# Cross-attention with LayerNorm: an input-ordered prologue, values placed by multiplication, the LayerNorm shift on GpSimd, another order in the epilogue

## The chip, the cores and the metric

The kernel runs on one NeuronCore of a Trainium2 chip. The metric is the device time of one execution in microseconds; the runs before the change gave 656.06, 656.39 and 652.27 (median 656.06). Engines are named as in the profile: PE is TensorE (PEld its weight loads), DVE VectorE, ACT ScalarE, POOL GpSimd, SP the engine that issues most DMAs.

## What is computed

Four batches of 2048 queries with 512 features attend to 77 context rows each; 16 heads of 32 features. gamma and beta are drawn at random.

```
qs = (x @ wq) in heads;  ks = (ctx @ wk) in heads;  vs = (ctx @ wv) in heads
scores = qs ks^T / sqrt(32);  scores = where(mask, -inf, scores)
attn = softmax(scores) @ vs
out = attn @ wo + x
result = (out - mean(out)) / sqrt(var(out) + 1e-5) * gamma + beta
```

## The kernel before

**Tiles and blocks.** 8192 query rows make 64 tiles of 128 rows, and two tiles make a block of 256 (32 blocks); a batch has 16 tiles. The order of every instruction is written out by hand: the loop `for u in range(NT + 8)` issues, in one turn u, pieces of different tiles. Each engine works through its own instructions strictly in that order.

**Precision.** A matmul operand in fp32 is split in two fp32r parts, high (a cast on ACT) and low (a subtraction, on DVE or GpSimd), and each product is three matmuls: high x high, high x low, low x high. `split` does it for weights and inputs.

**One turn u of the loop, in order.**
- `load_xT(b)` loads the transposed inputs of a later block (SP, and a casting DMA on GpSimd's queue); `load_x(u-5)` loads the residual rows.
- `shift` (L362, DVE): minus mean times reciprocal deviation, for the two tiles of a block, every second turn.
- `scores(u)`: 12 matmuls on PE (L249), then 16 DVE instructions (L252) that add the mask bias, negate and reduce, one per head, from PSUM.
- `av_evac` (odd u: ah on ACT L321, al on DVE L322), `q_evac` (qh on ACT L149, ql on DVE L150); at the end of a batch `kblocks` (kbh on ACT L174, kbl on DVE L175) puts the next batch's keys in a block-diagonal layout.
- `scale` (L372, ACT) for two finished tiles, then `exps(u)`: 16 exps on ACT (L266) with sums.
- `transp(u-1)`: a DVE transpose of the probabilities (L287); each second turn `regroup`: 12 DMAs on SP (L298) that place them as PT for the value products.
- `split_xT` (GpSimd L122), `affine` (GpSimd L376, L377: gamma and beta).
- `o_proj(u-6)` (PE L338), `av` (even u, PE L307: 32 small matmuls per block), `q_half` (PE L139: 24 matmuls), in that order on PE.
- `stats(u-6)`: residual add (L344), bn_stats (L346), aggregate (L351), variance plus epsilon (L357) on DVE and the power -1/2 on GpSimd (L358), for two tiles at once in odd turns.
- `normalise(u)`: reciprocal of the sums on DVE (L278), multiplication of the probabilities on GpSimd (L281).
- stores. The last four tiles (TAILV) are scaled by DVE (L369, L370) instead.

**Heads in pairs.** Probabilities of a pair of heads lie side by side, 154 columns padded to 160. Transposed in blocks of 32, head 1 of a pair begins 77 columns in, so its keys come out rotated; the value rows and the key order of odd heads must match that. vsb has 96 rows per batch: 77 keys and 19 more (TAIL_K) that repeat the tail for odd heads, and zero rows where a head has nothing.

**Prologue.** Inputs x and wq arrive in four chunks of 128 features, then ctx and wk, all on SP's queue. q of block 0 is computed by output group (each needs all four chunks), then the keys (`keys`), then the loop begins. Value weights are split by GpSimd. In turns 1 and 2 `values` computes the values of 308 context rows in three groups of up to 128 rows regardless of the batch, copies them from PSUM (ACT L189), and 16 small DMAs on SP (L196) place them in vsb, which GpSimd has set to zero (L386).

**Buffers.** PSUM has 8 banks, used in rotation by all matmul results. `o` tiles have 4 buffers, so stats of tile t waits for the store of tile t - 4; xtf has one buffer.

Of the kernel before, what the change touches and what calls it, by code (L numbers as in the profile page):

```python
# [40 lines left out]
def xattn_layernorm(  # L41
# [38 lines left out]
    bet = const.tile([P, D], F32, name="bet")  # L80
    mhalf = const.tile([P, 2], F32, name="mhalf")
    pbuf = [const.tile([P, NP, PW], F32, name=f"pbuf{i}") for i in range(NPB)]

    stage_a = sb.tile([P, 2, NC_D, D], F32, tag="PT", name="stage_a")
    stage_b = sb.tile([P, 2, NC_D, D], F32, tag="PT", name="stage_b")
    ctx_t = sb.tile([P, NC_D, NB * NK], F32, tag="B", name="ctx_t")
    ctx_f = [ctx_t[:, c] for c in range(NC_D)]
    ctx_2 = sb.tile([P, 2, NC_D, NB * NK], F32R, tag="B", name="ctx_s")
    ctx_s = [ctx_2[:, i] for i in range(2)]
    wvh = [sb.tile([P, D], F32R, tag="o", bufs=4, name=f"wvh{c}") for c in range(NC_D)]  # L90
    wv2 = [sb.tile([P, 2, D], F32R, tag=t, name=f"wvl{t}") for t in ("AH", "AL")]
    wvl = [wv2[c // 2][:, c % 2] for c in range(NC_D)]

    def wview(w, c):
        return w[c * P : (c + 1) * P, :]

    def split(hi, lo, src, eng=nc.vector):
        nc.scalar.copy(hi, src)
        eng.tensor_tensor(lo, src, hi.bitcast(F32), ALU.subtract)  # L99

# [4 lines left out]
    nmax, sums, bts, at, pas = {}, {}, {}, {}, {}  # L105
    xr, od, pos, mvs, rns = {}, {}, {}, {}, {}


    def load_xT(b):
        f = sb.tile([P, NC_D, BLK], F32, tag="xtf", bufs=1, name=f"xtf_{b}")  # L110
        h = sb.tile([P, NC_D, BLK], F32R, tag="xth", bufs=3, name=f"xth_{b}")
        nc.sync.dma_start(f, xT[b])
        if b == 1:
            nc.scalar.copy(h, f)
        else:
            nc.gpsimd.dma_start(h, xT[b])
        blk[b] = [h, f]

    def split_xT(b):
        h, f = blk[b]  # L120
        l = sb.tile([P, NC_D, BLK], F32R, tag="xtl", name=f"xtl_{b}")
        nc.gpsimd.tensor_tensor(l, f, h.bitcast(F32), ALU.subtract)  # L122
        blk[b] = [h, l]
# [28 lines left out]

    def keys():
        for m in range(NG):
            pk = bank(f"pk_{m}")
            ms = slice(m * P, (m + 1) * P)
            n = 0
            for c in range(NC_D):
                for w, i in ((woh, 0), (woh, 1), (wol, 0)):
                    nc.tensor.matmul(  # L160
                        pk[:, : NB * NK], w[:, c, ms], ctx_s[i][:, c, :], start=(n == 0), stop=(n == 11)
                    )
                    n += 1
            pkb = pk[:, : NB * NK].rearrange("p (b k) -> p b k", b=NB)
            nc.scalar.activation(kct[:, m, :, TAIL_K:], pkb, AF.Copy, scale=KSCALE)
            nc.scalar.copy(kct[:, m, :, :TAIL_K], kct[:, m, :, NK:])
            kblocks(0, slice(m, m + 1))

    def kblocks(b, ms=slice(0, NG)):
        for j in range(GH):  # L170
            q = slice(HD * j, HD * (j + 1))
            cs = slice(NK * j, NK * (j + 1))
            src = kct[q, ms, b, keys_of(j)]
            nc.scalar.copy(kbh[q, ms, cs], src)  # L174
            nc.vector.tensor_tensor(kbl[q, ms, cs], src, kbh[q, ms, cs].bitcast(F32), ALU.subtract)  # L175


    def values(r0):
        w = min(P, NB * NK - r0)
        pv = bank(f"pv_{r0}")  # L180
        n = 0
        for c in range(NC_D):
            for i, v in ((0, wvh), (0, wvl), (1, wvh)):
                nc.tensor.matmul(
                    pv[:w, :], ctx_s[i][:, c, r0 : r0 + w], v[c], start=(n == 0), stop=(n == 11)
                )
                n += 1
        vt = sb.tile([P, D], F32, tag="xr", bufs=3, name=f"vt_{r0}")
        nc.scalar.copy(vt[:w], pv[:w])  # L189
        for b in range(NB):  # L190
            lo, hi = max(r0, b * NK), min(r0 + w, (b + 1) * NK)
            for a, k0, k1, p0 in ((0, 0, NK, 0), (1, 0, NK - TAIL_K, 0), (1, NK - TAIL_K, NK, NK)):
                u0, u1 = max(lo, b * NK + k0), min(hi, b * NK + k1)
                if u0 < u1:
                    d0 = u0 - b * NK - k0 + p0
                    nc.sync.dma_start(  # L196
                        vsb[d0 : d0 + u1 - u0, b, :].rearrange("p (q a d) -> p q a d", a=2, d=HD)[:, :, a, :],
                        vt[u0 - r0 : u1 - r0, :].rearrange("p (q a d) -> p q a d", a=2, d=HD)[:, :, a, :],
                    )

    def load_wv():
        for c in range(NC_D):
            nc.sync.dma_start(stage_b[:, 0, c], wview(wv, c))
            nc.gpsimd.dma_start(wvh[c], wview(wv, c))
        for c in range(NC_D):
            nc.gpsimd.tensor_tensor(wvl[c], stage_b[:, 0, c], wvh[c].bitcast(F32), ALU.subtract)

# [17 lines left out]

    def mask_bias(b):
        mb, nz, m8 = bat[b]
        nc.vector.tensor_scalar(mb[:, :, TAIL_K:], m8, MASKED, None, ALU.mult)
        nc.vector.tensor_copy(mb[:, :, :TAIL_K], mb[:, :, NK:])

# [61 lines left out]
    def regroup(b):  # L292
        pt = pts[b] = sb.tile([P, 4, 2, NP * 2 * 32], F32, tag="PT", name=f"PT_{b}")
        bt = bts.pop(b).rearrange("p c q t r -> p c (q t r)")
        for c in range(3):
            src = bt[:, 2:3].to_broadcast((P, 2, NP * 2 * 32)) if c == 2 else bt[:, c : c + 4 : 3]
            for i in range(4):
                nc.sync.dma_start(pt[32 * c : 32 * c + 32, i], src[32 * i : 32 * i + 32])  # L298

# [41 lines left out]
    def stats(t):  # L341
# [10 lines left out]
        nz = bat[t // TPB][1]  # L352
        lone = t >= NT - 2
        if lone or tt == 1:
# [3 lines left out]
            nc.gpsimd.tensor_tensor(rn[:, 0, j], rn[:, 0, j], mhalf[:, j], ALU.pow)  # L358

    def shift(b):  # L360
        mv, rn = mvs[b], rns[b]
        nc.vector.scalar_tensor_tensor(rn[:, 1, :], mv[:, :, 0], -1.0, rn[:, 0, :], ALU.mult, ALU.mult)  # L362

# [18 lines left out]

    nc.gpsimd.memset(mhalf, -0.5)
    nc.gpsimd.memset(kbh.bitcast(F32), 0.0)
    nc.gpsimd.memset(kbl.bitcast(F32), 0.0)
    nc.gpsimd.memset(vsb, 0.0)  # L386
    for pb in pbuf:
# [9 lines left out]
    x0l = sb.tile([P, NC_D, BLK], F32R, tag="xtl", name="xtl_0")  # L397
    blk[0] = [x0h, x0l]
    for c in range(NC_D):
        nc.sync.dma_start(x0f[:, c], xT[0, :, c])  # L400
        nc.sync.dma_start(stage_a[:, 0, c], wview(wq, c))
        split(x0h[:, c], x0l[:, c], x0f[:, c], nc.gpsimd)
        split(wqh[:, c], wql[:, c], stage_a[:, 0, c])
    for c in range(NC_D):
        nc.sync.dma_start(ctx_f[c], ctxT[:, c].rearrange("p b k -> p (b k)"))
        nc.sync.dma_start(stage_a[:, 1, c], wview(wk, c))
    load_mask(0)
    for c in range(NC_D):
        split(ctx_s[0][:, c], ctx_s[1][:, c], ctx_f[c], nc.gpsimd if c == NC_D - 1 else nc.vector)
        split(woh[:, c], wol[:, c], stage_a[:, 1, c])  # L410
    q_half(0, 0)
    q_half(0, 1)
    q_evac(0, 0)
    q_evac(0, 1)
    load_xT(1)
    split_xT(1)
    load_wv()
    keys()
    mask_bias(0)
    mask_nan(0)  # L420

    evac = []

    load_xT(2)
    for u in range(NT + 8):
        odd = u % 2
# [6 lines left out]
        ln = [f for f in (u - 8, u - 7) if not odd and 0 <= f < NT - TAILV]  # L433
        if ln:
            shift(ln[0] // 2)
        if u < NT:
            scores(u)
        if odd and 0 <= (u - 5) // 2 < NBLK:
            av_evac((u - 5) // 2)
        for q in evac:  # L440
# [5 lines left out]
        if u < NT:  # L446
            exps(u, 0, 16)
        if 0 <= u - 1 < NT:
            transp(u - 1)
            if not odd:  # L450
                regroup((u - 1) // 2)
# [14 lines left out]
        b = (u - 4) // 2  # L466
        if not odd and 0 <= b < NBLK:
            av(b)
        for r in {1: (0, P), 2: (2 * P,)}.get(u, ()):
            values(r)  # L470
        evac = [(1, 0), (1, 1)] if u == 0 else [divmod(u + 3, 2)]
        evac = [q for q in evac if q[0] < NBLK]
# [4 lines left out]
        if u == 0:  # L477
            load_wo()
            split_xT(2)
        if 2 <= u <= 3:  # L480
            split_wo(2 * u - 4)
            split_wo(2 * u - 3)
        if u < NT:
            normalise(u)
        if o >= NT - TAILV and o < NT and (o % 2 or o >= NT - 2):
            for f in (o,) if o >= NT - 2 else (o - 1, o):
                scale(f)
                store(f)
        if odd and 0 <= u - 9 < NT - TAILV:
# [47 lines left out]
```

## Time and profile before

| what | before |
|---|---|
| median of three runs | 656.06 us |
| the profiled execution, its own time | 654.69 us |
| its span, first to last instruction | 652.9 us |
| mean granted PE clock | 0.955 |
| busy PE / DVE / ACT / POOL | 89% / 84% / 74% / 66% |
| L362, the shift on DVE: 30 instructions | 64.1 us busy, 20.1 us idle before |
| L281, normalise on GpSimd: 64 | 144.0 us busy, 2251 ns each |
| L358, power on GpSimd, 128x2: 33 | 24.5 us busy |
| q, 1536 matmuls of 256 columns (L139) | about 0.118 us apart at full clock |

A line of a timeline reads: start in us from the span's start, duration, engine (a q behind it means its queue of DMA issues), line of the kernel, operation, output <- inputs, shapes, count, and in brackets the idle time of the engine before it with what ended that. Windows give busy time of each engine in a stretch, then the granted clock of PE, the mean busy share of the 16 DMA engines, and GB/s. PE's busy time overlaps from one matmul to the next, so it overstates the load; distances between starts are better.

In the page's last three slices of 40 (some 49 us) PE's busy share falls to 7, 6 and 3 tenths, and the granted clock is 7 tenths.

### The profile page before, as it was taken

What the parts mean: (1) busy time and instruction counts of PE and PEld (TensorE: products, weight loads), DVE (VectorE), ACT (ScalarE), POOL (GpSimd) and SP (SyncE); (2) the same over time, 40 slices, a digit from 0 to 9 for tenths busy, and PEclk for the clock granted to TensorE, in tenths of its full rate; (3) what the DMA queues carried; (4) which work ended last, traced back from release to release, by engine and by line L of the source; (5) the groups of instructions that cost most, each with busy time, mean ns of one, the idle gap of its engine ahead of it and who ended that gap; (6) DMA issues with size and microseconds to landing.
All of it is one profiled execution on the core that took longest, in us unless ns stands there. A gap on an engine that the chain in (4) does not pass through costs nothing.

```text
span 652.9 us, 15185 instructions
## 1 busy us (share of the span) xinstructions
PE 580.5 (89%) x4190; PEld 489.9 (75%) x4190; DVE 550.9 (84%) x2631; ACT 483.7 (74%) x2293; POOL 431.3 (66%) x303
## 2 busy tenths in 40 slices
PE   8897499998999999998999999998999999998763
PEld 5896288887888888887888777887788777886442
DVE  5768188989998888999998888999998888898836
ACT  5499197777887777777887777777887777777710
POOL 5761456776578777776578777776578777765551
PEclk8899599998999999998999999998999999998777
DMA  8483976787757777787758777777757777556663
GB/s 264 144 259 66 235 198 172 208 233 209 201 142 209 208 208 209 207 230 213 193 135 224 209 208 205 212 224 222 195 140 212 210 209 208 143 147 162 169 171 112
DMA packets 68462, 126.11 MB, mean 193 GB/s; under 512 B 14746, under 2 KB 16282, under 8 KB 68378
## 3 DMA queue, kind: packets, MB, share of 16 engines
q1 hardware_dynamic: 62954, 107.31, 60.4%
q0 software_dynamic: 5424, 17.83, 8.9%
q8 instruction: 34, 0.56, 0.4%
q14 instruction: 50, 0.41, 0.2%
HBM read 57.36 MB, written 16.78 MB: 114 GB/s over the span
## 4 chain that ended last, share of the span: by engine, by line
DVE 53%; ACT 23%; PE 10%; issue 5%; POOL 4%; SPq 3%; DMA 2%; DVEq 0%; POOLq 0%; ACTq 0%
ACT pbuf L266 19%; DVE pbuf L252 12%; DVE rn L362 10%; DVE B L287 8%; DVE al L322 5%; PE pq L139 5%; DVE st L346 4%; POOL rn L358 4%; DVE o L344 3%; DVE ql L150 3%; ACT o L372 3%; SPq L298 2%; PE pa L307 1%; DVE kbl L175 1%; DVE nm L252 1%
## 5 line engine op out<-in xcount | busy, mean ns | idle before, releaser
L266 ACT ACTIVATE pbuf<-pbuf,nm 128x77 f32<-128x77 f32 x1024 | 352.1, 350 | 8.8 <-DVE nm L252 8.1
L266 ACT ACTIVATION_READ_ACCUMULATOR pbuf<-pbuf,nm 128x1 f32 x1024 | 194.9, 190 | 0.0
L281 POOL TENSOR_TENSOR pbuf<-pbuf,ri 128x1232 f32<-128x1232 f32 x64 | 144.0, 2251 | 55.5 <-DVE ri L278 51.0
L252 DVE CUSTOM_DVE_ANT_0 pbuf<-sc,mb 128x77 f32<-128x77 f32 x1024 | 164.9, 230 | 13.2 <-PE sc L249 13.2
L139 PE MATMUL pq<-xth,wqh 128*128 128x256 f32 x512 | 148.6, 290 | 20.7 <-DVE nm L252 19.3
L139 PE MATMUL pq<-xth,wql 128*128 128x256 f32 x512 | 146.0, 285 | 0.4 <-DVE wql L99 0.4
L139 PE MATMUL pq<-xtl,wqh 128*128 128x256 f32 x512 | 145.9, 285 | 0.0
L139 PEld LDWEIGHTS pq<-xth,wqh 128*128 128x128 f32 x512 | 98.7, 193 | 36.3 <-PE pa L307 29.3
L372 ACT ACTIVATE o<-o,rn 128x512 f32<-128x512 f32 x60 | 45.7, 808 | 106.9 <-DVE rn L362 106.9
L338 PE MATMUL po<-woh,ah 128*128 128x512 f32 x256 | 106.7, 417 | 7.5 <-DVE o L344 5.6
L338 PE MATMUL po<-woh,al 128*128 128x512 f32 x256 | 105.4, 412 | 2.5 <-DVE al L322 2.5
L338 PE MATMUL po<-wol,ah 128*128 128x512 f32 x256 | 104.7, 409 | 0.0
L287 DVE STREAM_TRANSPOSE B<-pbuf 128x1280 f32<-128x1280 f32 x64 | 96.0, 1500 | 8.0 <-POOL pbuf L281 7.9
L139 PEld LDWEIGHTS pq<-xtl,wqh 128*128 128x128 f32 x512 | 98.4, 192 | 1.8 <-POOL xtl L99 0.6
L139 PEld LDWEIGHTS pq<-xth,wql 128*128 128x128 f32 x512 | 98.3, 192 | 1.3 <-DVE wql L99 1.3
L358 POOL TENSOR_TENSOR rn<-rn,mhalf 128x2 f32<-128x2 f32 (+1 forms) x33 | 24.5, 743 | 111.7 <-DVE rn L357 111.7
L122 POOL TENSOR_TENSOR xtl<-xtf,xth 128x1024 fp32r<-128x1024 f32 x31 | 74.6, 2407 | 23.5 <-DMA xtf<-xT 11.4
L376 POOL TENSOR_TENSOR o<-o,gam 128x512 f32<-128x512 f32 x60 | 77.6, 1293 | 14.6 <-ACT o L372 14.6
L249 PE MATMUL sc<-kbl,qh 128*128 128x308 f32 x256 | 78.2, 305 | 6.7 <-DVE kbl L175 6.7
L307 PE MATMUL pa<-PT,vsb 96*32 96x256 f32 x1024 | 65.3, 398 | 19.9 <-DMA vsb<-vt 14.5
L252 DVE DVE_READ_ACCUMULATOR2_ANT nm<- 128x1 f32 x1024 | 82.3, 80 | 0.0
L377 POOL TENSOR_TENSOR o<-o,bet 128x512 f32<-128x512 f32 x60 | 78.9, 1315 | 4.7
(70 smaller groups left out, 976.3 us busy)
## 6 DMA issues: line engine op xcount, KB each, us to landing
PT<-B SPq DMA_DIRECT2D x384, 128.0 KB
xr<-x SPq DMA_DIRECT2D x64, 256.0 KB
out<-o SPq DMA_DIRECT2D x64, 256.0 KB
xtf<-xT SPq DMA_DIRECT2D x31, 512.0 KB
xth<-xT POOLq DMA_DIRECT2D x30, 512.0 KB, 4.6
stage_a<-wq SPq DMA_DIRECT2D x4, 256.0 KB
stage_a<-wk SPq DMA_DIRECT2D x4, 256.0 KB
stage_b<-wv SPq DMA_DIRECT2D x4, 256.0 KB
```

The costliest lines, as they stand in the source:

```text
L122: nc.gpsimd.tensor_tensor(l, f, h.bitcast(F32), ALU.subtract)
L139: nc.tensor.matmul(pq[:, i * BLK : (i + 1) * BLK], w[:, c, ms], r[:, c, :], start=(n == 0), stop=(n == 11))
L249: nc.tensor.matmul(sc[:, :GW], a[:, g, rs], k[:, g, :], start=(n == 0), stop=(n == 2))
L252: nc.vector.tensor_tensor_reduce(pb[:, h // 2, (h % 2) * NK : (h % 2 + 1) * NK], sc[:, j * NK : (j + 1) * NK], mb[:, t % TPB, keys_of(h)], ...
L266: nc.scalar.activation(pb[:, h // 2, (h % 2) * NK : (h % 2 + 1) * NK], pb[:, h // 2, (h % 2) * NK : (h % 2 + 1) * NK], AF.Exp, bias=nmax[t ...
L281: nc.gpsimd.tensor_tensor(pv, pv, rv.to_broadcast((P, NP, 2, NK)), ALU.mult)
L287: nc.vector.transpose(bts[b][:, :, :, tt, :].rearrange("p c q r -> p q c r"), pbuf[t % NPB].rearrange("p q (c r) -> p q c r", c=5),)
L307: nc.tensor.matmul(pas[b][g // 2][HD * j : HD * (j + 1), (g % 2) * BLK : (g % 2 + 1) * BLK], vsb[:, 2 * b // TPB, HD * h : HD * (h + 1)], ...
L338: nc.tensor.matmul(po, a[:, c, rs], w[:, c, :], start=(n == 0), stop=(n == 11))
L362: nc.vector.scalar_tensor_tensor(rn[:, 1, :], mv[:, :, 0], -1.0, rn[:, 0, :], ALU.mult, ALU.mult)
L376: nc.gpsimd.tensor_tensor(o, o, gam, ALU.mult)
L377: nc.gpsimd.tensor_tensor(o, o, bet, ALU.add)
```

## The change

- **Prologue, loads.** ctx comes in two DMAs on ACT's queue, with 96 rows per batch (the 19 tail keys repeated, made on the host), ahead of the weights of the keys on SP. Block 1's inputs are loaded early, without the casting DMA.
- **Prologue, order of work.** q of block 0 accumulates chunk by chunk in four banks, as chunks arrive. The keys accumulate in two halves of the chunks. All low parts of splits go to DVE (four of x and one of ctx were on GpSimd, as were block 1's and the value weights'). q_half(1, 0) moves ahead of the loop. The evacuation of the keys alternates between ACT and DVE, and the tail keys are taken from PSUM by DVE. Before the loop, the mask bias is made for the first tile alone; the other tiles' follows in turn 0, mask_nan in turn 1.
- **Values.** One group of 96 rows per batch (turns 1, 2, 3 and 3), evacuated by two DVE multiplications with a column of ones and zeros (`vm`), which `value_rows` makes. No DMAs, no zeroed vsb.
- **Shift.** Two 128x2 multiplications on GpSimd right behind the power (times the reciprocal deviation, times -1), in `stats`.
- **Epilogue.** The last four tiles get their own power each, and are scaled and stored each in its own turn. Half of the last regroup's 12 DMAs are issued by ACT. `av` of the last block and its evacuation move from turn 66 and 67 to turn 67, behind `o_proj(61)`.

```diff
@@ stats
-        lone = t >= NT - 2
+        lone = t >= NT - TAILV
...
             nc.gpsimd.tensor_tensor(rn[:, 0, j], rn[:, 0, j], mhalf[:, j], ALU.pow)
-
-    def shift(b):
-        mv, rn = mvs[b], rns[b]
-        nc.vector.scalar_tensor_tensor(rn[:, 1, :], mv[:, :, 0], -1.0, rn[:, 0, :], ALU.mult, ALU.mult)
+            if not lone:
+                nc.gpsimd.tensor_tensor(rn[:, 1, :], mv[:, :, 0], rn[:, 0, :], ALU.mult)
+                nc.gpsimd.tensor_tensor(rn[:, 1, :], rn[:, 1, :], mneg, ALU.mult)
@@ regroup
-                nc.sync.dma_start(pt[32 * c : 32 * c + 32, i], src[32 * i : 32 * i + 32])
+                eng = nc.scalar if b == NBLK - 1 and i % 2 else nc.sync
+                eng.dma_start(pt[32 * c : 32 * c + 32, i], src[32 * i : 32 * i + 32])
@@ values
+    def values(b):
+        pv = bank(f"pv_{b}")
         n = 0
         for c in range(NC_D):
             for i, v in ((0, wvh), (0, wvl), (1, wvh)):
+                nc.tensor.matmul(pv[:NK2, :], ctx_s[c][i][:, b, :], v[c], start=(n == 0), stop=(n == 11))
                 n += 1
+        vd[b] = pv
+
+    def values_evac(b):
+        pv = vd.pop(b)[:NK2].rearrange("p (q a d) -> p q a d", a=2, d=HD)
+        for a in range(2):
+            nc.vector.tensor_scalar(
+                vsb[:, b].rearrange("p (q a d) -> p q a d", a=2, d=HD)[:, :, a], pv[:, :, a], vm[:, a, 0:1], None, ALU.mult
+            )
@@ prologue
+    for c in range(0, NC_D, 2):
+        nc.scalar.dma_start(ctx_f[:, c : c + 2], ctxT[:, c : c + 2])
     for c in range(NC_D):
         nc.sync.dma_start(stage_a[:, 1, c], wview(wk, c))
     load_mask(0)
+    load_xT(1, False)
+    value_rows()
+    pq0 = [bank(f"pq_0_{m}") for m in range(NG)]
     for c in range(NC_D):
+        split(x0h[:, c], x0l[:, c], x0f[:, c])
+        split(wqh[:, c], wql[:, c], stage_a[:, 0, c])
+        for m in range(NG):
+            for n, (w, r) in enumerate(((wqh, x0h), (wqh, x0l), (wql, x0h))):
...
+    for c in range(NC_D):
+        split(ctx_s[c][0], ctx_s[c][1], ctx_f[:, c])
         split(woh[:, c], wol[:, c], stage_a[:, 1, c])
+    for m in range(NG):
+        split(qd[0][0][:, m], qd[0][1][:, m], pq0[m][:, :BLK])
+    pks = [bank(f"pk_{m}") for m in range(NG)]
+    for m in range(NG):
+        keys_part(pks, m, (0, 1))
+    for m in range(NG):
+        keys_part(pks, m, (2, 3))
+    nc.scalar.copy(blk[1][0], blk[1][1])
+    split_xT(1)
+    q_half(1, 0)
+    mask_bias(0, slice(0, 1))
+    load_wv()
+    for m in range(NG):
+        keys_evac(pks, m)
     load_xT(2)
@@ the loop
-    for u in range(NT + 8):
+    for u in range(NT + 7):
...
-        if not odd and 0 <= b < NBLK:
+        if not odd and 0 <= b < NBLK - 1:
             av(b)
-        for r in {1: (0, P), 2: (2 * P,)}.get(u, ()):
-            values(r)
+        if u == NT + 3:
+            av(NBLK - 1)
+            av_evac(NBLK - 1)
+        for v in {1: (0,), 2: (1,), 3: (2, 3)}.get(u, ()):
+            values(v)
...
-        if o >= NT - TAILV and o < NT and (o % 2 or o >= NT - 2):
-            for f in (o,) if o >= NT - 2 else (o - 1, o):
-                scale(f)
-                store(f)
+        if NT - TAILV <= o < NT:
+            scale(o)
+            store(o)
```

## The prediction

> **What bounds the kernel now.** I read the page first, then the windows, the timeline of one block, the chain of waits and the last 30 us. PE is 89% busy, but three different things set the time.
>
> In the middle (103 to 614 us) the LayerNorm line L357 recurs every 17.78 us, one block of two tiles. The timeline of one such turn, all engines, exps and score rows left out:
>
> ```profile
> 361.06 0.16 DVE L357 TENSOR_TENSOR rn<-mv,nz 128x2 f32<-128x2 f32 x1
> 361.30 0.71 POOL L358 TENSOR_TENSOR rn<-rn,mhalf 128x2 f32<-128x2 f32 x1 [2.78 <-DVE rn L357]
> 361.99 2.24 POOL L281 TENSOR_TENSOR pbuf<-pbuf,ri 128x1232 f32<-128x1232 f32 x1
> 362.05 2.20 DVE L362 SCALAR_TENSOR_TENSOR rn<-mv,rn 128x2 f32<-128x2 f32 x1 [0.66 <-POOL rn L358]
> 364.29 1.52 ACT L372 ACTIVATE o<-o,rn 128x512 f32<-128x512 f32 x2 [3.36 <-DVE rn L362]
> 365.03 0.35 PE L139 MATMUL pq<-xth,wqh 128*128 128x256 f32 x1 [1.00 <-DVE nm L252]
> ```
>
> L362 computes 128x2 numbers and takes 2.20 us; it ends (364.25) with the GpSimd instruction beside it (364.23). Late in the trace, with GpSimd idle, the same instruction is short:
>
> ```profile
> 623.80 0.16 DVE L362 SCALAR_TENSOR_TENSOR rn<-mv,rn 128x2 f32<-128x2 f32 x1 [0.81 <-POOL rn L358]
> ```
>
> So the turn is a loop: L357, pow on GpSimd, L362 held until L281 is done, two scales on ACT, 16 exps on ACT (to about 371.2), reciprocal, then the odd tile's scores, al, ql, transpose and statistics on DVE (7.4) to the next L357 at 378.84. PE only loses 1.0 us per turn, after the probability-value products. PE's own floor shows early, where it still ran ahead: scores begin at 102.81, 119.55 and 136.28, a turn of 16.74.
>
> In the prologue (windows; columns: PE, PEld, DVE, ACT, POOL busy, clock, DMA) PE stands still from 60.4 to 75.05, and the chain of waits gives the reason: SP issues the regroup, then the copies of the values.
>
> ```profile
> 65.00:70.00 5.00, 0.00 (x0) 0.00 (x0) 0.00 (x0) 1.87 (x12) 2.53 (x2) 0.50 0.96 255
> 70.00:75.00 5.00, 0.00 (x0) 0.00 (x0) 1.65 (x2) 0.00 (x0) 3.70 (x3) 0.50 1.10 229
> ...
> 72.98 0.85 SPq L196
> 73.87 1.11 DMA vsb<-vt
> 75.05 3.64 PE pa L307 x32
> ```
>
> In the epilogue PE waits for the last regroup, and the residual add of tile 62 (third row) for a store (timeline):
>
> ```profile
> 618.37 7.93 SPq L298 DMA_DIRECT2D PT<-B  x12
> 628.13 3.64 PE L307 MATMUL pa<-PT,vsb 96*32 96x256 f32 x32 [5.09 <-DMA PT<-B]
> 642.29 0.69 DVE L344 TENSOR_TENSOR o<-po,xr 128x512 f32<-128x512 f32 x1 [0.71 <-DMA out<-o]
> ```
>
> The sum is made against the profiled execution: 654.69 us, span 652.9, so 1.8 lies around it. The median of the runs is 1.4 higher; I add that at the end.
>
> **Shift on GpSimd.** Removed from DVE: 30 L362 (64.1 us) and the 20.1 us that DVE waited for them. On the loop, L362 with its gap is 2.24. Added on GpSimd between pow and normalise: two 128x2 multiplies, each behind the one before (gap between dependent GpSimd instructions: L376 to L377, 0.07). Their price isn't in the trace. Above: pow on the same shape, 0.71, and at worst 1.14 (L358's longest, beside a DVE instruction of two inputs). Below: the 128x2 memset, 0.10. The fixed part of a GpSimd tensor_tensor from 128x256 (0.98) and 128x512 (1.29) is 0.67. I take 0.65, nearest to that and to pow: 2 x 0.72 = 1.44, turn 17.78 - 2.24 + 1.44 = 16.98; with 0.10 it would be 15.9, where PE's 16.74 takes over; with 1.14, 17.96. Allowing for a cheaper multiply than pow I use 16.95. L357 recurs 28 times between 103.51 and 613.59: 28 x 0.83 = 23 (ends -5 and 29).
>
> Who waits for the multiplies: normalise (L281) is queued behind them, so the odd tile's transpose starts at about 4.6 after L357; DVE, now done with the even scores and ql at 3.5, idles 1 us there, then has its statistics done at 7.6, before the reciprocal can run (exps end at 0.24 + 0.71 + 1.44 + 1.55 + 5.4 = 9.3). GpSimd's busy time per turn goes from 13.2 to 14.6 of 17; its affine pairs end at 10.7, the even tile's normalise at 12.9, and the transpose asks at 13.8. That cover is 0.9 us; beyond it each us is on the loop.
>
> Batch boundaries: three turns of 18.87 (mask bias, L228 and L229) and three of 21.0 (mask_nan, and the L175 key blocks, 2.35). DVE's even half now has about 1.9 us to spare, so 1.1 + 0.9 can vanish; the key blocks lie in the odd half and stay. I take 4.5 in all (0 to 6).
>
> **Prologue.** Values: 16 SP copies, 3 ACT copies and a GpSimd memset (1.8, early, free) go; two DVE multiplies per batch from PSUM (512 elements like L150, about 0.7 for both halves) come, and 48 matmuls take the place of 36 (12 x 0.23 = 2.8 on PE). The stall of 14.6 goes, and with it the half clock after it: 32 products took 3.57 until the next group, 1.86 later on: 1.7.
>
> What is late next at av(0)? transp(1), SP's 12 issues (7.7) and landing (2.4): about 41 + 10 = 51, against PE at 56; covered by 5.
>
> Order of arrival: q(0) runs by input chunk, so about 12 matmuls remain after the last chunk instead of 36. Key weights still land at 14.3 (the last woh cast waits for them). Add cast 0.6, subtraction 0.7, half of the keys 24 x 0.143 and the moved q_half(1,0), 2.8: 22.5. But DVE now has all subtractions (five left GpSimd) and part of the key evacuation, some 20 us from 4, so the last key block comes near 26 (before: 28.0). Then 24 instead of 48 q matmuls before scores(1): 30 against 36.87. The first 12 value matmuls wait for DVE's four subtractions (0.69 each, moved from GpSimd): scores(2) 37.5 against 46.95; scores(3) 44.8 against 54.22; 24 value matmuls in the next turn: scores(4) 55 against 58.73. So 3.8 is left, and with 14.6 + 1.7 the prologue gives 20. Ends: 13 (order brings nothing, the 2.8 counts) and 24. The ctx loads, 0.17 MB larger, go to ACT's queue beside x and wq; at the 340 GB/s of 5 to 10 us they can delay the first chunks by 2.3 us, hidden while key weights are the last to land, otherwise on the path. x(1) is loaded ahead of the value weights on SP and of block 2; nothing waits for those before the first values.
>
> Small moves of the prologue, at no cost: the mask bias of the other 15 tiles (L228 and L229, 3.0) and mask_nan (1.9) go behind the first scores, on DVE, which then only waits for exps(0) and exps(1), 5.5 each; uncovered they would be 4.9. Key blocks in another order and tails taken from PSUM cost DVE what they spare ACT (0.26 x 4). value_rows, a dozen memsets and a transpose, runs before the first input lands at 3.6.
>
> A rule weighed: the clock. The windows show 0.50 after 65 us. The Trainium skill, "TensorE: Matmul & The Clock Gate", HAM oscillation, says that idle gaps over about 3.4 us bring half rate. By it new gaps under that cost nothing, and PE's wait at the first scores could cost one cold window (an estimate from its figures: up to 1.7 us).
>
> **Epilogue.** Behind L357 at 613.59 the multiplies delay normalise and transp(63) by 1.4. The 12 regroup issues go half to ACT, which is idle then. Row: at 622 to 628 the DMA engines are 90% busy at 199 GB/s with one issuer, so issuing faster can save about 10% of 7.4, 0.8; if the issue time were all, 3.8. I take 1. o_proj(61) moves ahead of av(31), under the wait; PE is 2.8 earlier. But statistics(61) sit on DVE behind al(31), which waits for av(31): 633.1 instead of 636.28. stats(62) still waits for store(58), which SP issues behind store(61); so 3.2 - 0.4 is left: 3 (0 to 7).
>
> A rule speaks against the split: "DMA: Bandwidth & Descriptors", Rules for kernel authors, says that spreading DMAs over issuing engines doesn't help bandwidth and saves issue time alone. The 90% row sides with it. By the rule alone, were issue time the limit, the 1 us would be 3.8; with the engines the limit, 0.
>
> **Sum.** 654.7 - 23 - 4.5 - 20 - 3 = 604.2, and 1.4 to the median: 605.6. PE's floor pulls a little the other way (a turn of 16.74 gives 6 more); I say 604.
>
> **The rivals.**
> - The turn hardly shortens (8%): normalise, pushed back, makes transposes the late ones, using up the 0.9 us of cover. The 51 us of GpSimd's waits for ri speak against it. Then only prologue, epilogue and little else: 656 - 20 - 3 - 3 = 630.
> - The prologue moves its stall (8%): DVE, with GpSimd's subtractions, or the regroup becomes late; 13 or less of 20: 612. For: DVE is near full until 26 us. Against: SP is free of copies.
> - Slower (3%): the multiplies are the new stall, at L362's own 2.2 each when DVE works beside them. Turn 17.78 - 2.24 + 4.5 = 20.0, 28 x 2.3 = 64 on top, less 20 and 3: 697. It decides from 1.55 us each, where 28 x (2 x 1.62 - 2.24) = 28 eats the rest. pow's 0.71, beside DVE's reciprocal, speaks against it.
> - Values are placed, but something else of those 14.6 stays (no change, 2%).
>
> **How the numbers follow.** Forecast 79%. Its range: steady part 16 to 35, prologue 13 to 24, epilogue 0 to 7, not all at one end: 591 to 622. Adding the second rival it holds; the first (630) lies outside, with the slower one. Telling 1% from no change is about what this kernel's spread of 0.6% allows. Faster 0.95, same 0.02, slower 0.03.
>
> **What would show it.** L357 recurring at 16.7 to 17.1; no L362; two 128x2 multiplies of 0.6 to 0.7 ahead of L281; no PE gap after the products; no gap at 60 us, scores(5) near 60; a clock of 0.5 only at the start and the last av; last L344 group by 640. Wrong if a turn stays above 17.5, if the first av waits for PT, or if L281 ends the transposes' waits.

## The result and the profile after

| | before | after |
|---|---|---|
| median | 656.21 us (652.27 to 656.39, 4 runs) | 595.37 us (594.32 to 596.33, 4 runs) |
| profiled execution, its span | 652.9 us | 592.5 us |
| mean granted PE clock | 0.955 | 0.981 |

The ratio after to before is 0.9085 (95% interval 0.9047 to 0.9124). The forecast was 604, range 591 to 622.

The page of the changed kernel: busy time of each engine with its share of the span, then the chain of waits that ended last, by engine and by line.

```profile
PE 564.5 (95%) x4202; PEld 482.0 (81%) x4202; DVE 500.5 (84%) x2640; ACT 482.1 (81%) x2286; POOL 427.7 (72%) x354
...
PE 79%; DVE 6%; DMA 5%; SPq 4%; ACT 2%; issue 2%; POOL 2%; POOLq 0%; ACTq 0%
PE pq L140 26%; PE po L352 26%; PE sc L262 16%; PE pa L321 9%; SPq L312 4%; DMA PT<-B 2%; PE pv L201 2%; DVE kbl L182 2%; DMA stage_a<-wk 1%; ACT pbuf L279 1%; DMA ctx_f<-ctxT 1%; DVE al L336 1%; POOL o L390 1%; POOL rn L372 0%; DMA xr<-x 0%
```

PE now carries 79% of the chain, in its four loops of matmuls, and hardly anything of the LayerNorm is left in it. One turn of the loop, where L362 stood before (timeline of the changed kernel, start, duration, engine, line):

```profile
355.62 0.16 DVE L371 TENSOR_TENSOR rn<-mv,nz 128x2 f32<-128x2 f32 x1
...
355.86 0.71 POOL L372 TENSOR_TENSOR rn<-rn,mhalf 128x2 f32<-128x2 f32 x1 [2.14 <-DVE rn L371]
...
356.65 0.19 POOL L374 TENSOR_TENSOR rn<-mv,rn 128x2 f32<-128x2 f32 x1
...
356.92 0.20 POOL L375 TENSOR_TENSOR rn<-rn,mneg 128x2 f32<-128x2 f32 x1
...
357.07 2.26 POOL L294 TENSOR_TENSOR pbuf<-pbuf,ri 128x1232 f32<-128x1232 f32 x1
...
357.15 1.52 ACT L385 ACTIVATE o<-o,rn 128x512 f32<-128x512 f32 x2 [1.66 <-POOL rn L375]
```

The two multiplications take 0.19 and 0.20 us, not 0.65, and the scales start 1.53 us after L371 (before: 3.23). To divide the gain I take the power on GpSimd (L358 before, L372 after) as a marker: it runs once per block, in both kernels.

| stretch | before | after | gain | forecast |
|---|---|---|---|---|
| start to the first power | 103.75 | 89.55 | 14.2 | 20 |
| first power to the 29th, 28 turns | 510.08 | 463.60 | 46.5 | 27.5 |
| of it 28 regular turns | 28 x 17.78 = 497.8 | 28 x 16.52 = 462.6 | 35.3 | 23 |
| of it what the boundaries add | 12.2 | 1.0 | 11.2 | 4.5 |
| 29th power to the end | 39.07 | 39.35 | -0.3 | 3 |

Sum 60.4, which is 652.9 - 592.5. The pitch of the marker is 16.52 three times, 19.56 at the end of a batch (key blocks), and then 16.07 five times: the loop over ACT, DVE and GpSimd has a length of 16.07 of its own, so it runs behind PE, whose turn is 16.52, and makes up after each boundary what it lost. PE itself loses 0.7 us at a boundary.

Prologue (windows of the changed kernel: busy PE, PEld, DVE, ACT, POOL, clock, DMA share, GB/s); PE stood still here before:

```profile
65.00:70.00 5.00, 5.00 (x43) 5.00 (x43) 4.86 (x37) 5.00 (x25) 3.74 (x2) 1.00 0.49 113
70.00:75.00 5.00, 4.65 (x26) 3.80 (x25) 4.18 (x27) 4.98 (x28) 2.81 (x2) 1.00 0.91 203
```

Epilogue (timeline of the changed kernel; ACTq and SPq are the engines' queues of DMA issues):

```profile
558.17 5.23 ACTq L312 DMA_DIRECT2D PT<-B  x6
558.20 4.98 SPq L312 DMA_DIRECT2D PT<-B  x6
563.50 1.07 ACT L335 CAST ah<-pa 128x512 fp32r<-128x512 f32 x2 [7.55 <-DMA PT<-B]
564.14 0.79 PE L352 MATMUL po<-woh,ah 128*128 128x512 f32 x1 [5.76 <-ACT ah L335]
```

The casts of block 30, which need only value products that were long done, start when ACT has issued its six DMAs. The bracket names the DMA; ACT's own issues are what stands in front. PE waits 5.76 us for them.

### The profile page after: what moved, and what is told of

Read it like the earlier page. It is cut to its first block, busy times and chain, and to the rows that moved or that the text cites. A ratio compares the mean times of both kernels' runs of the same rounds, so it can differ in the third digit from the quotient of the medians.

```text
span 592.5 us, 15276 instructions
## 1 busy us (share of the span) xinstructions
PE 564.5 (95%) x4202; PEld 482.0 (81%) x4202; DVE 500.5 (84%) x2640; ACT 482.1 (81%) x2286; POOL 427.7 (72%) x354
## 4 chain that ended last, share of the span: by engine, by line
PE 79%; DVE 6%; DMA 5%; SPq 4%; ACT 2%; issue 2%; POOL 2%; POOLq 0%; ACTq 0%
PE pq L140 26%; PE po L352 26%; PE sc L262 16%; PE pa L321 9%; SPq L312 4%; DMA PT<-B 2%; PE pv L201 2%; DVE kbl L182 2%; DMA stage_a<-wk 1%; ACT pbuf L279 1%; DMA ctx_f<-ctxT 1%; DVE al L336 1%; POOL o L390 1%; POOL rn L372 0%; DMA xr<-x 0%
## 5 line engine op out<-in xcount | busy, mean ns | idle before, releaser
L294 POOL TENSOR_TENSOR pbuf<-pbuf,ri 128x1232 f32<-128x1232 f32 x64 | 144.4, 2257 | 31.4 <-DVE ri L291 25.4
L140 PE MATMUL pq<-xth,wqh 128*128 128x256 f32 x496 | 142.0, 286 | 0.0
L140 PE MATMUL pq<-xtl,wqh 128*128 128x256 f32 x496 | 139.0, 280 | 0.0
L140 PE MATMUL pq<-xth,wql 128*128 128x256 f32 x496 | 138.9, 280 | 0.0
L352 PE MATMUL po<-woh,ah 128*128 128x512 f32 x256 | 103.5, 404 | 7.3 <-ACT ah L335 7.3
L300 DVE STREAM_TRANSPOSE B<-pbuf 128x1280 f32<-128x1280 f32 x64 | 96.4, 1506 | 16.0 <-POOL pbuf L294 13.7
L352 PE MATMUL po<-woh,al 128*128 128x512 f32 x256 | 102.8, 402 | 4.0 <-DVE al L336 4.0
L140 PEld LDWEIGHTS pq<-xth,wqh 128*128 128x128 f32 x496 | 93.8, 189 | 13.3 <-issue 11.9
L372 POOL TENSOR_TENSOR rn<-rn,mhalf 128x2 f32<-128x2 f32 (+1 forms) x34 | 24.9, 733 | 98.4 <-DVE rn L371 98.4
L140 PEld LDWEIGHTS pq<-xth,wql 128*128 128x128 f32 x496 | 94.9, 191 | 0.0
L140 PEld LDWEIGHTS pq<-xtl,wqh 128*128 128x128 f32 x496 | 93.9, 189 | 1.2
L262 PE MATMUL sc<-kbh,qh 128*128 128x308 f32 x256 | 77.9, 304 | 1.1 <-ACT kbh L181 1.1
L262 PE MATMUL sc<-kbh,ql 128*128 128x308 f32 x256 | 77.7, 304 | 0.0
```

Of the source, the lines that this page charges most:

```text
L140: nc.tensor.matmul(pq[:, i * BLK : (i + 1) * BLK], w[:, c, ms], r[:, c, :], start=(n == 0), stop=(n == 11))
L262: nc.tensor.matmul(sc[:, :GW], a[:, g, rs], k[:, g, :], start=(n == 0), stop=(n == 2))
L294: nc.gpsimd.tensor_tensor(pv, pv, rv.to_broadcast((P, NP, 2, NK)), ALU.mult)
L300: nc.vector.transpose(bts[b][:, :, :, tt, :].rearrange("p c q r -> p q c r"), pbuf[t % NPB].rearrange("p q (c r) -> p q c r", c=5),)
L352: nc.tensor.matmul(po, a[:, c, rs], w[:, c, :], start=(n == 0), stop=(n == 11))
```

## The experiments

Line numbers in the profiles of experiments are those of each kernel's own code. Ratios are to the kernel before.

### The shift: where its price comes from

**1. Only the shift moved.** The kernel before, with

```
+                nc.gpsimd.tensor_tensor(rn[:, 1, :], mv[:, :, 0], rn[:, 0, :], ALU.mult)
+                nc.gpsimd.tensor_tensor(rn[:, 1, :], rn[:, 1, :], mneg, ALU.mult)
...
-            shift(ln[0] // 2)
```

> The kernel before, with the shift alone moved to GpSimd. Theory (the held L362 sets the turn of 17.78, and without it PE does at 16.5): 28 turns lose the 46.5 us that they lost in the changed kernel, 656 - 46.5 = 610; no other stage moves (first av still at 75). Rival (the shorter turn also needs the earlier start and the freer DVE of the new prologue): turns settle at 17 or more, 630.

Measured 608.06 us (606.25 to 608.63), ratio 0.9272 (0.9246 to 0.9297). First power to the 29th: 462.2, so the shift alone makes the whole gain of the middle (47.9 of 510.08); the turns are 16.45, 19.56 and 16.07 (16.52, 19.56 and 16.07 in the changed kernel). The rival that the turn hardly shortens falls.

**2. The shift left on DVE, with one tensor input.**

```
-        nc.vector.scalar_tensor_tensor(rn[:, 1, :], mv[:, :, 0], -1.0, rn[:, 0, :], ALU.mult, ALU.mult)
+        for j in range(2):
+            nc.vector.tensor_scalar(rn[:, 1, j : j + 1], mv[:, j, 0:1], rn[:, 0, j : j + 1], -1.0, ALU.mult, ALU.mult)
```

> The kernel before, with the shift still on DVE behind the power, but as two instructions of one tensor input each (mean, times a per-partition pointer to the reciprocal deviation, times -1). Theory (L362 is held by L281 because it reads two tensors from SBUF): about 0.1 to 0.2 us each, turn 16.5, 610, as with GpSimd. Rival (any small DVE instruction that follows the power beside L281 is held): 2.2 us stay, 656.

Measured 613.64 us (612.88 to 614.29), ratio 0.9361 (0.9339 to 0.9383). Its timeline:

```profile
340.45 2.25 POOL L281 TENSOR_TENSOR pbuf<-pbuf,ri 128x1232 f32<-128x1232 f32 x1
340.51 0.33 DVE L363 TENSOR_SCALAR rn<-mv,rn 128x1 f32<-128x1 f32 x2 [0.66 <-POOL rn L358]
```

Same engine, same moment, same GpSimd instruction beside it, but the second operand is a pointer to a scalar per partition instead of a second tensor: both take 0.33 us together, and neither is held. So DVE isn't slow at this and GpSimd isn't quick; the instruction with two tensors from SBUF waits until the GpSimd instruction is over. The opcode changed as well, but experiment 5 shows another opcode with two tensors (a subtraction) held in the same way. The Trainium skill, "SBUF — State Buffer", Who interferes with whom, states this rule (two SBUF inputs contend with a GpSimd instruction that reads SBUF; at most one, outside the modes that use two ports, doesn't); 0.16 alone, 2.20 beside L281 and 0.33 for the pair here agree with it. The remaining 5.6 us to experiment 1 go with a turn of 16.73 instead of 16.45. No wait of PE makes it: PE runs through such a turn without a gap, only its matmuls are a little slower (24 q matmuls in 2.82 to 2.96 us, in experiment 1 in 2.74 to 2.85, the granted clock 1.00 in both). Why is open.

**3. The changed kernel with the shift back on DVE**, as the single instruction with two tensors.

```
-                nc.gpsimd.tensor_tensor(rn[:, 1, :], mv[:, :, 0], rn[:, 0, :], ALU.mult)
-                nc.gpsimd.tensor_tensor(rn[:, 1, :], rn[:, 1, :], mneg, ALU.mult)
...
+            nc.vector.scalar_tensor_tensor(rn[:, 1, :], mv[:, :, 0], -1.0, rn[:, 0, :], ALU.mult, ALU.mult)
```

> The changed kernel with the shift back on DVE as before. Theory: turns of 17.78, 18.9 and 21.0 at the batch boundaries return, 594.3 + 46.5 = 641. Rival (DVE's new slack absorbs the held instruction): below 615.

Measured 641.31 us (640.93 to 641.48), ratio 0.9783 (0.9761 to 0.9805). Turns of 17.78, 18.84 and 20.97 are back, and the 28 turns take 509.9. The shift is worth the same 46 to 48 us with and without the rest: it adds up.

### The prologue

**4. The values by DMA again**, in the new order of the prologue.

```
-            nc.vector.tensor_scalar(
-                vsb[:, b].rearrange("p (q a d) -> p q a d", a=2, d=HD)[:, :, a], pv[:, :, a], vm[:, a, 0:1], None, ALU.mult
+        nc.scalar.copy(vt[:NK2], pv[:NK2])
+        for a, k0, k1 in ((0, 0, NK), (1, 0, NK - TAIL_K), (1, NK, NK2)):
+            nc.sync.dma_start(
...
```

> The changed kernel, whose values go through SBUF and three DMAs on SP per batch again (12 in all, vsb zeroed by GpSimd), but still batch by batch. Theory (the stall of 14.6 us came from SP issuing 13 slow copies, about 1.4 us each, ahead of the first regroup, and three behind it): now only three copies lie ahead of the first regroup and PE is not there yet, so little returns: 596 to 601. Rival (any placing by DMA costs the stall): 609.

Measured 605.94 us (604.7 to 606.82), ratio 0.9243 (0.9215 to 0.9272): 10.6 more than the changed kernel, beyond the theory (601) and nearer to the rival (609). SP's issues in its timeline, and PE's line for the second value products:

```profile
57.74 3.74 SPq L210 DMA_DIRECT2D vsb<-vt  x3
...
62.96 9.48 SPq L210 DMA_DIRECT2D vsb<-vt  x6
72.55 8.41 SPq L315 DMA_DIRECT2D PT<-B  x12
```

```profile
85.14 3.64 PE L324 MATMUL pa<-PT,vsb 96*32 96x256 f32 x32 [10.73 <-DMA xr<-x]
```

Each copy takes 1.2 to 1.6 us of SP's queue. The first value products come on time (60.69, in the changed kernel 60.93); the stall moves to the second, behind six copies and a regroup, and PE idles 10.7 us (2 in the changed kernel). The bracket names the load of the residual rows that SP issues right behind the regroup; the products read only PT and vsb. The multiplications are worth 11.3 of the prologue's 14.2 (first power at 100.87 against 89.55). Twelve copies instead of sixteen, one group per batch, don't remove the stall; they move it.

**5. The low part of block 2 on DVE.** In the changed kernel not all low parts of the prologue are on DVE: GpSimd still makes this one.

```
-        eng = nc.vector if b == 1 else nc.gpsimd
+        eng = nc.vector if b <= 2 else nc.gpsimd
```

> The changed kernel with one instruction of the prologue moved: the low part of the inputs of block 2, on GpSimd at 24.81 for 2.38 us, is made by DVE. Theory: it holds one key block's subtraction on DVE (two inputs from SBUF) for 2.43 instead of 0.23 us, and the first scores end by that much late; taken away, the scores of tile 1 come 2.2 us earlier, 32.6, and most of it arrives at the end: 593 to 594. Rival: DVE pays the subtraction itself (some 0.7 to 1.4 us) at a place where it is needed, or another wait takes its place: 595 to 596.

Measured 591.84 us (591.3 to 593.27), ratio 0.9047 (0.9031 to 0.9063). First the changed kernel's rows, GpSimd and DVE, then DVE's of this one (four subtractions of key blocks):

```profile
24.81 2.38 POOL L123 TENSOR_TENSOR xtl<-xtf,xth 128x1024 fp32r<-128x1024 f32 x1 [0.73 <-DMA xtf<-xT]
24.85 3.22 DVE L182 TENSOR_TENSOR kbl<-kct,kbh 32x77 fp32r<-32x77 f32 x4
```

```profile
24.81 1.07 DVE L182 TENSOR_TENSOR kbl<-kct,kbh 32x77 fp32r<-32x77 f32 x4
```

It is the mechanism of L362 once more, in a place where I didn't look for it. Taken away, the scores of tile 1 begin at 30.95 instead of 34.77 and the first power comes at 86.49 instead of 89.55: 3.06, more than the 2.2 of the instruction itself. The rest goes with PE's clock: two gaps of 1.4 us in the scores of tile 0 shrink to one of 0.8, and a granted clock of 0.5 from about 31 to 34 us is gone; the 24 q matmuls behind those scores take 2.73 us instead of 4.36. Windows in these q matmuls (the number before the last two is the clock), the changed kernel and this one:

```profile
32.00:34.00 2.00, 2.00 (x11) 2.00 (x11) 2.00 (x10) 2.00 (x13) 0.00 (x0) 0.50 1.15 387
```

```profile
30.00:32.00 2.00, 2.00 (x18) 2.00 (x18) 2.00 (x8) 2.00 (x13) 0.00 (x0) 1.00 0.00 0
```

### The epilogue

The medians of experiments 6 to 8 lie within 2 us of the changed kernel's, and they come from different comparisons. So I compare a distance inside the profiled executions that holds nothing of the prologue, from the 28th power to the end: 54.8 us in the changed kernel (537.68 to 592.5).

**6. The old epilogue** in the changed kernel.

```
-                eng = nc.scalar if b == NBLK - 1 and i % 2 else nc.sync
...
-        if u == NT + 3:
-            av(NBLK - 1)
-            av_evac(NBLK - 1)
...
+        if o >= NT - TAILV and o < NT and (o % 2 or o >= NT - 2):
```

> The changed kernel with the old epilogue alone (old order of the last turns, last regroup on SP alone). Theory: the new epilogue brought nothing (39.35 us from the power of tiles 56 and 57 to the end, against 39.07 before), because what it gains on the regroup is lost to the issues that ACT makes ahead of the casts of block 30: the same time as the changed kernel's 595.4, 594 to 597. Rival: the steady part now leaves the epilogue in a different state, and the new order still hides its 3 us: 598 to 600.

Measured 596.74 us (596.48 to 598.2), ratio 0.9117 (0.9102 to 0.9133); distance 55.8. By this the new epilogue is worth about 1 us, not 3.

**7. The last regroup on SP alone**, the rest of the new epilogue kept: `nc.sync.dma_start(pt[...])` for all 12.

> The changed kernel with all 12 issues of the last regroup on SP, everything else of the new epilogue kept. Theory (ACT's six issues of 0.6 to 0.9 us keep the casts of block 30 from 558 to 563.5, and PE waits 5.8 us for them): the casts run near 556, o_proj(60) and o_proj(61) are done by 565.5, the regroup takes 7.5 instead of 5.7 and av(31) starts near 568.4 instead of 572.65: 591 to 592. Rival (the shorter regroup is what counts, and the casts are only late for it): av(31) comes 2 us later, 596 to 598.

**8. The split kept, the casts of block 30 ahead of it.**

```
-        if odd and 0 <= b < NBLK - 1:
+        if odd and 0 <= b < NBLK - 2:
...
+        if u == NT:
+            av_evac(NBLK - 2)
+            regroup(NBLK - 1)
```

> The changed kernel with the evacuation of block 30 ahead of the last regroup in ACT's queue, so that the split of the issues stays and the casts don't wait behind it. Theory: the casts run near 556, and with a split regroup (5.7 us) av(31) can start near 566 instead of 572.65: 588 to 590, some 2 us better than all issues on SP. Rival (the transfers, not the issues, set the length of the regroup): as with all issues on SP, 591 to 592. If the casts are not the cause, 595.

Measured 593.61 us (593.2 to 594.98; 0.9069, 0.9053 to 0.9084) and 593.65 us (592.84 to 594.79; 0.9067, 0.9051 to 0.9082); distances 53.7 and 53.0. Issues and the value products that wait for them, first SP alone, then split:

```profile
558.32 8.62 SPq L311 DMA_DIRECT2D PT<-B  x12
...
568.97 2.48 PE L320 MATMUL pa<-PT,vsb 96*32 96x256 f32 x32 [3.24 <-DMA PT<-B]
```

```profile
559.76 7.11 ACTq L312 DMA_DIRECT2D PT<-B  x6
559.79 6.42 SPq L312 DMA_DIRECT2D PT<-B  x6
...
571.11 3.64 PE L321 MATMUL pa<-PT,vsb 96*32 96x256 f32 x32 [5.43 <-DMA out<-o]
```

From the first issue to the value products it is 10.65 us with one issuer and 11.35 with two. An issue then takes 1.1 to 1.2 us (6.42 and 7.11 for six) instead of 0.72 (8.62 for twelve), with the DMA engines at full share (1.0 in the windows from 562 on; 0.66 to 0.87 from 560 to 568 with SP alone). So the split brings the value products no earlier, and the medians are the same. The bracket of the split names a store, so which transfer ended that wait isn't shown. The rule that the prediction weighed (the Trainium skill, "DMA: Bandwidth & Descriptors", Rules for kernel authors: spreading DMAs over issuing engines doesn't help bandwidth) agrees, and the 0.8 to 3.8 us that I allowed for are not there. The casts behaved as the theory had it (555.96 on SP alone, forecast 556; value products at 568.97, forecast 568.4), but of the 3.7 us that the value products came earlier only 1.1 arrived, and both medians lie above their theories (591 to 592, 588 to 590). The chain of waits of the kernel on SP alone shows what came next:

```profile
567.67 3.11 DMA out<-o
...
570.98 0.70 DVE o L357
...
572.89 1.01 POOL rn L371
573.96 0.63 issue
574.59 0.70 DVE al L335
```

The sum of tile 60 waits for the store of tile 56, which SP issues behind the regroup; the low part of block 31 stands behind it on DVE.

**9. That store and the loads out of the way**, with experiments 5 and 7 kept.

```
+        tag, n = (("xth", 3), ("xtf", 1), ("xtl", 2), ("xtl", 2))[t - NT + 4]
+        return sb.tile([P, D], F32, tag=tag, bufs=n, name=f"o_{t}")
...
+            if u == NT - 2:
+                load_x_tail()
```

> The changed kernel with the low part of block 2 on DVE, the last regroup on SP alone, and what waited behind that regroup on SP taken out of its way: the residual rows of the last four tiles are loaded two turns earlier and their outputs have buffers of their own, so the sums of tiles 60 and 63 wait neither for a store nor for a load. Theory (the store behind the regroup is what now sets the epilogue): the sum of tile 60 comes 8 us earlier, the low part of block 31 starts near 572.2 instead of 574.6 (then held by the power of tile 60, behind the gamma and beta of tiles 58 and 59 on GpSimd), and tile 63 saves 1.4 us of waiting: 593.6 - 3.1 - 2.4 - 1.4 = 586.7, so 585.5 to 588. Rival (these waits only hide others, the value products and the half clock): 590 to 591.

Measured 587.1 us (586.87 to 590.56), ratio 0.8979 (0.8957 to 0.9002); distance 50.4, 3.3 below experiment 7. The theory holds. What is late now, in this kernel's chain of waits:

```profile
567.24 1.28 POOL o L402
568.52 0.53 POOL rn L384
...
569.07 0.75 DVE o L395
569.82 0.61 DVE al L335
```

The power of tile 60 waits behind gamma and beta of tiles 58 and 59 on GpSimd, the scale of tile 60 behind the power, and the low part behind the scale.

**10. The low part ahead of the scales of 60 and 61**, tiles 58 and 59 scaled by DVE.

```
-TAILV = 4
+TAILV = 6
...
+        if o == NT - 3:
+            av_evac(NBLK - 1)
+            for f in (NT - 4, NT - 3):
+                scale(f)
...
```

> As tail_buffers, and on DVE the low part of block 31 is put ahead of the scales of tiles 60 and 61, with tiles 58 and 59 scaled by DVE as well (no gamma and beta on GpSimd for them). Theory (after the store, GpSimd's gamma and beta are the next wait): the low part follows the value products at once, near 571 to 572: 1 to 1.5 us less than tail_buffers, 585 to 586. Rival (four more scales of 0.75 us make DVE the wait, or the products are no earlier): same as tail_buffers or above.

Measured 589.92 us (585.4 to 593.91), ratio 0.8989 (0.8956 to 0.9022): inconclusive, since single runs lie 8.5 us apart. In the profiled run (593.91) the granted clock is 0.5 from 562 to 568.5, and the 22 matmuls of the projections of tiles 60 and 61 that follow a PE gap of 3.1 us take 8.13 us; the clock also fell in the prologue, from 74 to about 81. And the rival has its part too: four scales of 0.75 us (572.8 to 575.9) keep the low part waiting.

**11. PE kept busy during the regroup.**

```
+            for i in range(16):
+                nc.tensor.matmul(pw, warm[:, :P], warm, start=True, stop=True)
             av(NBLK - 1)
```

> As tail_order, with 16 matmuls on zeros (3.4 us at full clock) on PE between the projection of tile 61 and the last value products, in the time in which PE waits for the regroup. Theory (PE stands still for 3.6 us there, and its products and projections then run at half clock): 32 value products in 1.9 instead of 2.4 to 3.6 us, the two projections in 2.8 each: 2 to 3 us less than tail_order, 582.5 to 584. Rival (the clock isn't what counts, or falls all the same): no difference.

Measured 588.82 us (587.66 to 590.48), ratio 0.8995 (0.8974 to 0.9016). The distance is 49.5, 0.9 below experiment 9 (54.0 in the profiled run of experiment 10, with its half clock), the 22 matmuls take 5.33 and the value products 1.91 us, but the median is no better than experiment 9's: in the profiled run (587.66) the clock fell in the prologue. The theory's 582.5 to 584 is missed.

**12. PE kept busy in both waits**: 9 such matmuls ahead of the second value products as well, and the last residual rows loaded one block earlier.

```
+            if b == 1:
+                for i in range(9):
+                    nc.tensor.matmul(pw, warm[:, :P], warm, start=True, stop=True)
```

> As tail_warm, with 9 more matmuls on zeros ahead of the second value products of the prologue, where PE waits 2.3 us for a regroup, and with the residual rows of the last four tiles loaded one block earlier, ahead of the store that the sum of tile 58 waits for (559.4 in tail_order, 557.5 in tail_warm). Theory: after that wait of 2.3 us the clock falls to half for some 3 us in some executions and not in others (in three of the eight profiled runs on this kernel that have the wait and the values without DMA), at 1.6 us each time; with the wait filled it stays at full speed in the profiled run, scores(7) begins 11.2 us or less after scores(6), and the median is 1 to 3 us below tail_warm's: 585 to 587.5, with a smaller spread. Rival (the falls of the clock have other causes, and the spread is elsewhere): median 588 to 589.

Measured 585.88 us, ratio 0.8936 (0.8914 to 0.8957), and five runs within 585.82 to 586.02. The text above miscounts: with experiment 3 there are nine profiled kernels with this wait, and the clock fell in five (experiments 3, 6, 8, 10 and 11). Windows at that place: the changed kernel, experiment 8, and this one (3 us earlier, with experiment 5 in it).

```profile
78.00:80.00 2.00, 2.00 (x25) 1.59 (x17) 1.33 (x4) 1.74 (x8) 0.44 (x1) 1.00 0.87 307
```

```profile
76.00:78.00 2.00, 1.45 (x28) 1.07 (x32) 1.79 (x3) 2.00 (x13) 0.00 (x0) 0.95 1.00 335
78.00:80.00 2.00, 2.00 (x17) 1.19 (x9) 1.56 (x4) 1.68 (x7) 0.21 (x1) 0.50 0.99 361
80.00:82.00 2.00, 2.00 (x14) 2.00 (x14) 0.00 (x0) 0.00 (x0) 2.00 (x1) 0.70 1.09 197
```

```profile
74.00:76.00 2.00, 2.00 (x36) 1.20 (x25) 1.97 (x3) 2.00 (x13) 0.00 (x0) 1.00 1.05 374
```

The same wait of 2.3 to 2.4 us from one matmul's start to the next (PE busy 0.56 and 0.65 of 2.00 before it) is followed by 0.50 in one kernel and by 1.00 in the other. The scores of tile 7 begin 11.26 us after those of tile 6 in the changed kernel, 12.91 in experiment 8, and 11.31 here (I had asked for 11.2). With the wait filled, the spread of several us is gone. The experiment changes two things, but the earlier loads bring little: the distance is 49.3 instead of 49.5, while the first power comes at 86.67 instead of 88.23. This is the fastest version of the study, 70 us below the kernel before.

## Why the prediction was right, and where its sizes were off

**The total: in the range partly by luck.** The steady part gave 46.5, above the 16 to 35 from which the range was made, and the epilogue -0.3, below its 0 to 7. Had prologue and epilogue brought their 20 and 3, the median would have been 654.7 - 46.5 - 20 - 3 + 1.4 = 586.6, below the range. Errors in opposite directions kept it inside.

**What bounds the kernel: right.** The loop through L362 set the turn, and PE was next. Experiment 1 makes the whole gain of the middle by those two lines. One sign named for being wrong did come: normalise now ends the transposes' waits (L300 idles 16.0 us, 13.7 of them for L294, about 0.35 once per turn; in the middle of the kernel before, none). It is small, and PE sets the turn all the same.

**Shift, 23 forecast, 35.3 measured.** The mechanism held; the term mis-sized is the multiplication. I took 0.65, near pow and the fixed part of large GpSimd instructions; it is 0.20, near the row of the memset (0.10), which I had as the lower end. With 0.20 and a pitch of 0.27 my own sum gives 17.78 - 2.24 + 0.54 = 16.08, and the loop runs at 16.07. Then PE's floor decides, as the text said for a cheap multiplication. That floor I read as 16.74 from two turns behind the prologue; it is 16.52. PE had no waits in those two turns either: its matmuls were slower (24 q matmuls in 2.82 to 2.96 us, against 2.83 to 2.84), as in experiment 2, and why stays open.

**Boundaries, 4.5 forecast, 11.2 measured.** I counted the slack of DVE inside the turn. But with the loop at 16.07 under a PE of 16.52, 0.45 us per turn is free, and the five turns behind a boundary make up most of the 3 us that its marker loses. The turns of 18.87 vanish altogether. This follows from the mis-sized multiplication: at 16.95 the loop would have had nothing to make it up with.

**Prologue, 20 forecast, 14.2 measured (range 13 to 24).** The stall before the first value products goes, as predicted, but experiment 4 shows that the new order does that with DMA copies too; what the multiplications save is the stall that would then stand before the second ones. Of the 5.8 missing, 3.1 are the subtraction on GpSimd that I left in the sum at no cost (experiment 5): I said that the last key block comes near 26, and it came at 30.0, 27.8 without the hold. (The terms ahead of that add up to 21.8, not 22.5; the sum went by 26, so nothing hung on it.) "Scores(1) 30" was 34.77, and 30.95 with it repaired. PE also waits 2.3 us for the regroup before the second value products, a transfer whose cover I had worked out for the first only. That and about 1.1 us already there at the scores of tile 4 (56.08 in experiment 5, forecast 55) are 3.4, more than the other 2.7; where 0.7 came back wasn't looked into.

**Epilogue, 3 forecast, about 1 by experiment 6.** The failed step is "the 12 regroup issues go half to ACT, which is idle then". ACT wasn't idle: the casts of block 30 were due, and its queue is in order. And the split itself brings the value products no earlier (experiments 7 and 8). By the marker the stretch is 0.3 longer than before.

**The clock.** "By it new gaps under that cost nothing" was wrong here. Two gaps of 1.4 us with two matmuls between them, in the scores of tile 0, and a single one of 2.3 us ahead of the second value products, there in five profiled kernels of nine, were followed by half rate: mostly for some 3 us, with 1.5 to 1.7 us lost, and in experiment 10 for some 7 us, with 3.3 lost. Yet a wait of 2.9 us in the epilogue of experiment 9 (PE from 555.40 to 558.34) was followed by a clock of 1.00. So the length of one wait doesn't decide it, and the figure weighed there (the Trainium skill, "TensorE: Matmul & The Clock Gate", HAM oscillation: idle gaps over about 3.4 us) is no safe bound; experiment 12 is the measurement that decides, with one profiled execution and five runs.

**The rivals.** None happened. The second (the prologue moves its stall) described half of what did: the stall at 60 us went and a smaller one appeared at 74 us (2.3 us), but the total stayed within the main range.

## What to carry to other kernels

Before an instruction of DVE that reads two tensors from SBUF is called short, look at what GpSimd runs beside it: if it is held, a pointer to a scalar in place of one tensor or a move to GpSimd frees it, and every other such pair in the kernel deserves the same look. A DMA issue costs its engine's queue, so list what is queued behind it on that engine before moving it there, and don't expect more issuers to shorten a transfer whose engines are already mostly busy. When single runs of one kernel scatter by a few us, look for PE waits of some 2 us on its path and try whether filling them ends it.

## What the hardware showed that I had not expected

- A GpSimd multiplication of 128x2 numbers takes 0.20 us, a power on the same shape 0.71, though large GpSimd instructions extrapolate to 0.67 at zero length.
- The granted clock can fall after a PE wait of 2.3 us, or after two of 1.4 close together; for the same wait of 2.3 us it fell in five profiled executions of nine. With it filled, the spread of a kernel's runs went from 2.8 us (experiment 11) to 0.2.
- A profile names a DMA as the releaser where an engine's own queue of DMA issues was in front (ACT in the epilogue). Its six issues took 0.59 to 0.94 us each there, and up to 1.41 in experiment 8, against mostly 0.59 (one of 1.40) when SP issues alone.
